# Channel mix of the last layer woven into the last attention unit

## The chip, the cores and the metric

One core of a Trainium2 chip runs the whole program. The metric is the device time of one execution in microseconds (us). TensorE (PE) multiplies matrices, VectorE (DVE), ScalarE (ACT) and GpSimd (POOL) work on tiles, SyncE (SP) issues DMAs.

## The reference

Two layers on x, 2048 tokens by 128 channels. Each layer has a modulated layer norm, attention with a gated residual, another modulated layer norm and a feed-forward part with a gated residual. Layer 0 has 16 heads of 8 and a mixture of 16 experts. Layer 1 has causal attention with 8 heads of 16 and a channel mix:

```
h = layernorm(x) * (1 + cb) + sb
h_prev = h shifted by one token (zeros in front)
xr = mu_r * h + (1 - mu_r) * h_prev
xk = mu_k * h + (1 - mu_k) * h_prev
x = x + gb * sigmoid(xr @ W_r.T) * (square(relu(xk @ W_k.T)) @ W_v.T)
```

The channel mix is the last thing computed; its result is the output. It goes along tokens only by the shift by one, so 512 tokens of it need the attention of those tokens, and one column of the block in front of them.

## The kernel before

x stays in SBUF as 16 tiles of 128 tokens by 128 channels. Work on tokens goes by 4 blocks (0 to 3) of 512 tokens (`QB`), each of 4 tiles (`TB`). Transposed activations lie as 128 channels by 2048 tokens.

Attention (`attention`) goes by units: a unit is one block of 512 queries and one group of 4 heads. Layer 1 has 8 units (0 to 7), two for each block; units 6 and 7 belong to block 3. A unit has two passes.

- The first pass (`first_pass`) multiplies queries by keys into a PSUM tile of 128 x 1024 (L411), and VectorE takes the maximum from it (L415; on the diagonal L420, which masks). At its end the negated maxima are made (L426, L436, L437), transposed on TensorE (L444) and copied (L445).
- The second pass (`second_pass`) multiplies keys by queries again (L476), adds the negated maxima with a second product (L482), ScalarE takes the exponential out of PSUM (L486), on the diagonal GpSimd clears the later tokens (L489), and TensorE weighs the values with it (L502) into a PSUM bank `av`.

The first pass of the next unit runs ahead within the second pass of the present one (`look_ahead`), so the last unit, 7, has no first pass beside it. Both passes take their score tiles from one ring of three (`ps_s`). Of the two further banks, one is the `av` of the unit and the other (`other_bank`) serves every small product. What a unit leaves behind, `normalise`, goes into a list `late` of pieces: `divide` (transposes L533, reciprocal and product L537, L538), and after the second unit of a block `turn_back` (L545, L548) and `project` (four products L554 and the addition to x, L558). A piece is taken from `late` at every second step of a second pass, and at every step in the last unit. A step is one score tile; unit 7 has 32.

Behind attention comes the channel mix for all four blocks. `layernorm_T` takes the statistics of 16 tiles (L180, L181), one square root on ScalarE (L182), reciprocal (L183), 16 normalised tiles (L189), 16 transposes (L191), and four evictions on ScalarE (L192). Then, for each block, two scalings on ScalarE (L1208), two additions of the shifted tile on VectorE (L1210), products with W_r and W_k (L1213, L1215), the sigmoid on ScalarE (L1217), the maximum with 0 on VectorE (L1219), the square on GpSimd (L1221), the product with W_v (L1223), times the sigmoid (L1225), times the gate on GpSimd (L1226), four transposes back (L265), the addition to x (L267) and a DMA of 256 KB to the output (L1228).

Inside layer 1's attention and the channel mix, the order of instructions on each engine is decided by the framework's scheduler when the program is built, from the order in which the kernel calls them and from what depends on what. Every engine then runs its list in order, and an instruction that waits holds up all behind it on that engine.

Of the kernel before, what the change touches and what calls it, by code (L numbers as in the profile page):

```python
# [19 lines left out]
P = 128  # L20
# [23 lines left out]
def two_layers(ctx: ExitStack, tc: tile.TileContext, a: dict, out: bass.AP):  # L44
# [126 lines left out]
    def layernorm_T(hT, off, scale, shift, tagp):  # L171

        with tc.tile_pool(name=tagp + "_s", bufs=1) as one, \
                tc.tile_pool(name=tagp + "_w", bufs=4) as wp, \
                tc.tile_pool(name=tagp + "_p", bufs=4, space=PSUM) as pp:
            stats = one.tile([P, NT, nc.vector.BN_STATS_DIM], F32, name=tagp + "stats", tag="stats")
            mv = one.tile([P, NT, nc.vector.BN_AGGR_DIM], F32, name=tagp + "mv", tag="mv")
            rstd = one.tile([P, NT], F32, name=tagp + "rstd", tag="rstd")
            for t in range(NT):
                nc.vector.bn_stats(stats[:, t, :], x[:, t, :])  # L180
                nc.vector.bn_aggr(mv[:, t, :], stats[:, t, :])  # L181
            nc.scalar.activation(rstd, mv[:, :, 1], AF.Sqrt, bias=eps)  # L182
            nc.vector.reciprocal(rstd, rstd)  # L183
            for b in range(NB):
                ps = pp.tile([P, QB], F32, name=f"{tagp}ps{b}", tag="ps")
                for i in range(TB):
                    t = b * TB + i
                    xn = wp.tile([P, P], F32, name=f"{tagp}xn{t}", tag="xn")
                    nc.vector.tensor_scalar(xn, x[:, t, :], mv[:, t, 0:1], rstd[:, t:t + 1],  # L189
                                            ALU.subtract, ALU.mult)  # L190
                    nc.tensor.transpose(ps[:, i * P:(i + 1) * P], xn, ident)  # L191
                nc.scalar.activation(hT[:, off + b * QB:off + (b + 1) * QB], ps, AF.Identity,  # L192
                                     bias=shift, scale=scale)

# [66 lines left out]

    def add_to_x(b, t, ps):

        for i in range(TB):
            nc.tensor.transpose(ps[:, i * P:(i + 1) * P], t[:, i * P:(i + 1) * P], ident)  # L265
        xb = x[:, b * TB:(b + 1) * TB, :]
        nc.vector.tensor_tensor(xb, xb, ps.rearrange("p (t c) -> p t c", c=P), ALU.add)  # L267
# [49 lines left out]
    def attention(layer, hT, ngrp, dk, scale, causal, kvp, begin, prepare, wq, bq, folded, ended,  # L317
# [23 lines left out]
        with ExitStack() as s:  # L341
# [116 lines left out]
            def second_pass(u):  # L458
# [48 lines left out]
                def steps():  # L507
# [10 lines left out]
                    weights.append(lambda: (last(), late.extend(normalise(u, av))))  # L518
# [3 lines left out]
            def normalise(u, av):  # L522
# [28 lines left out]
                def project():  # L551
                    ps = other_bank()
                    for i in range(TB):
                        nc.tensor.matmul(ps[:, i * P:(i + 1) * P],  # L554
                                         attended[b][:, i * P:(i + 1) * P], folded[0],
                                         start=True, stop=True)
                    xb = x[:, b * TB:(b + 1) * TB, :]
                    nc.vector.tensor_tensor(xb, xb, ps.rearrange("p (t c) -> p t c", c=P), ALU.add)  # L558
# [50 lines left out]
            for u in range(len(units)):  # L609
# [3 lines left out]
                for n in range(1, size + 1):  # L613
# [5 lines left out]
                    if n == LEAD and u + 1 == len(units):  # L619
# [327 lines left out]
    with ExitStack() as s:  # L947
# [214 lines left out]
        while len(shared) > 1:  # L1162
# [22 lines left out]

    attention(1, h2, H1 // HG, D1, float(P) ** -0.5, True, pool1,
              lambda ep, pp, stacks: ((lambda st: kS1), (lambda kt, head: vA1[:, kt, :]), qS1),
              ready1, wq1, None, folded1, lambda bank: [], lambda late, *_: late)
    a1.close()


    h = hpool.tile([P, HOFF + T], F32, name="hT3", tag="hT")
    nc.gpsimd.memset(h[:, 0:HOFF], 0.0)
    layernorm_T(h, HOFF, m[:, 4:5], m[:, 3:4], "ln3")
    ov = out.rearrange("(t p) c -> p t c", p=P)
    with ExitStack() as s:
        rp = s.enter_context(tc.tile_pool(name="mixc", bufs=1))
# [96 lines left out]
```

## Time and profile before

| | |
|---|---|
| median of 3 runs | 1252.55 us (1251.54 to 1255.32) |
| the profiled execution | 1254.59 us, its span 1252.9 us |
| TensorE busy, share of the span | 92% |
| VectorE busy | 75% |
| ScalarE busy | 62% |
| GpSimd busy | 8% |
| granted TensorE clock, mean | 0.944 |
| unit 7 begins, by its first L476 | 1170.2 us |
| last L502 of unit 7 ends | 1209.55 us |
| last addition to x ends | 1249.2 us |

Times in the profile are from the start of the span. An engine is busy while an instruction runs on it; the number behind an operation is the time of one or, with x and a count, of a run of them. The idle time in brackets is that of the engine just before, with the instruction that ended it.

### The profile page before, as it was taken

Reading aid. Unit: us, or ns where it says so; the run is one execution under the profiler, and the core shown is the slowest. Engines: PE = TensorE matmul, PEld = TensorE weight load, DVE = VectorE, ACT = ScalarE, POOL = GpSimd, SP = SyncE. Lnnn points to the kernel's source line nnn. Section 1 sums busy time; section 2 is a strip of 40 time slices with the busy share of each in tenths; the row PEclk is TensorE's granted clock in tenths of the full one; section 3 lists DMA queues with packets and bytes.
Section 4 is the critical chain, followed back from the end, with each engine's and each line's share of the span. In section 5 each row is a group of like instructions: output and inputs, shape, how many; then the busy total and the mean of one; then the engine's idle time right before and its main releaser. Section 6 shows DMA issues by size and latency. Waiting matters only on the chain.

```text
span 1252.9 us, 22356 instructions
## 1 busy us (share of the span) xinstructions
PE 1156.8 (92%) x9230; PEld 523.6 (42%) x9230; DVE 943.9 (75%) x1462; ACT 780.3 (62%) x853; POOL 94.4 (8%) x157
## 2 busy tenths in 40 slices
PE   4579999999999999999999999979978989999985
PEld 2233434444343443443344333447734444444432
DVE  3888898889889889889889983343378788897134
ACT  6107777777777777777777778743333455656763
POOL 2002000000000000000000000320232011110113
PEclk9658999999999999999999999999977899999987
DMA  4841010203220213110000000032210101000001
GB/s 122 112 52 35 2 52 1 70 27 77 69 69 12 59 36 98 38 52 2 1 3 2 1 2 2 20 122 76 66 45 7 35 1 35 1 1 2 2 1 34
DMA packets 63094, 45.22 MB, mean 36 GB/s; under 512 B 6608, under 2 KB 56912, under 8 KB 62480
## 3 DMA queue, kind: packets, MB, share of 16 engines
q1 hardware_dynamic: 60224, 40.37, 13.2%
q0 software_dynamic: 1024, 2.10, 0.6%
q10 hardware_dynamic: 1744, 1.32, 0.6%
q8 instruction: 73, 1.20, 0.4%
q14 instruction: 29, 0.24, 0.1%
HBM read 9.88 MB, written 21.95 MB: 25 GB/s over the span
## 4 chain that ended last, share of the span: by engine, by line
PE 82%; DVE 10%; ACT 4%; issue 1%; DMA 1%; POOL 1%; ACTq 0%; POOLq 0%; DVEq 0%
PE a0bank L502 24%; PE a0p L476 17%; PE a0p L411 13%; PE a1bank L502 5%; PE a1p L476 4%; DVE a0mx L415 3%; DVE a1mx L415 2%; PE a1p L411 2%; PE a1p L482 2%; PE sg L991 2%; DVE a1masked L420 2%; ACT a0e L486 1%; PE gu L1043 1%; PE a0bank L533 1%; PE sum L979 1%
## 5 line engine op out<-in xcount | busy, mean ns | idle before, releaser
L415 DVE TENSOR_REDUCE a0mx<-a0p 128x2 f32<-128x1024 f32 x512 | 624.0, 1225 | 75.9 <-PE a0p L411 66.5
L486 ACT ACTIVATE a0e<-a0p 128x1024 f32<-128x1024 f32 x512 | 522.6, 1025 | 171.9 <-PE a0p L476 146.2
L502 PE MATMUL a0bank<-a0e,vA 128*32 128x256 f32 x4096 | 333.4, 392 | 0.8 <-ACT a0e L486 0.8
L411 PE MATMUL a0p<-kS,a0qS 64*128 64x512 f32 x1024 | 248.1, 480 | 24.7 <-DVE a0mx L415 13.0
L476 PE MATMUL a0p<-a0qS,kS 64*128 64x512 f32 x1024 | 260.6, 498 | 0.0
L486 ACT ACTIVATE a1e<-a1p 128x1024 f32<-128x1024 f32 (+3 forms) x160 | 143.1, 897 | 97.6 <-PE a1p L482 92.3
L476 PEld LDWEIGHTS a0p<-a0qS,kS 64*128 64x128 f32 x1024 | 97.3, 184 | 204.5 <-issue 128.7
L411 PEld LDWEIGHTS a0p<-kS,a0qS 64*128 64x128 f32 x1024 | 100.3, 192 | 109.4 <-ACT a0e L486 56.8
L502 PEld LDWEIGHTS a0bank<-a0e,vA 128*32 128x32 f32 x4096 | 86.4, 108 | 137.9 <-issue 124.4
L415 DVE TENSOR_REDUCE a1mx<-a1p 128x2 f32<-128x1024 f32 x96 | 115.8, 1222 | 17.8 <-PE a1p L411 17.2
L502 PE MATMUL a1bank<-a1e,vA 128*32 128x256 f32 (+1 forms) x1152 | 96.9, 385 | 0.4 <-POOL a1e L489 0.4
L476 PE MATMUL a1p<-a1qS,kS 64*128 64x512 f32 (+3 forms) x320 | 76.3, 463 | 4.9 <-DVE a1mx L415 3.7
L411 PE MATMUL a1p<-kS,a1qS 64*128 64x512 f32 (+3 forms) x320 | 67.7, 422 | 11.2 <-DVE a1mx L420 4.4
L420 DVE CUSTOM_DVE_ANT_0 a1masked<-a1p,later 128x128 f32<-128x128 f32 (+3 forms) x128 | 62.6, 489 | 13.4 <-PE a1p L411 7.5
L799 POOL DMA_INDIRECT sent<-hs,row_i x16 | 15.9, 995 | 712.6 <-DVE ln11xn L252 689.5
L482 PE MATMUL a1p<-a1mT,a1ones 64*128 64x512 f32 (+3 forms) x320 | 62.2, 375 | 0.0
L476 PEld LDWEIGHTS a1p<-a1qS,kS 64*128 64x128 f32 x320 | 31.5, 189 | 61.6 <-issue 32.3
L411 PEld LDWEIGHTS a1p<-kS,a1qS 64*128 64x128 f32 x320 | 32.2, 195 | 39.5 <-DVE a1mx L420 11.5
L489 POOL TENSOR_SCALAR_AFFINE_SELECT a1e<-a1e 128x256 f32<-128x256 f32 x64 | 26.0, 406 | 255.4 <-ACT a1e L486 255.4
L502 PEld LDWEIGHTS a1bank<-a1e,vA 128*32 128x32 f32 x1152 | 25.8, 109 | 42.8 <-issue 32.6
L445 ACT CAST a0mT<-a0bank 8x512 fp32r<-8x512 f32 x16 | 9.2, 576 | 45.4 <-PE a0bank L444 45.4
L482 PEld LDWEIGHTS a1p<-a1mT,a1ones 64*128 64x128 f32 x320 | 32.2, 193 | 2.3 <-issue 1.7
(340 smaller groups left out, 718.2 us busy)
## 6 DMA issues: line engine op xcount, KB each, us to landing
sent<-blank SPq DMA_DIRECT2D x68, 256.0 KB
kS<-a0qS SPq DMA_DIRECT2D x28, 128.0 KB
wgu_sb<-in_gate_up SPq DMA_DIRECT2D x1, 2048.0 KB
a0qS<-a0qh SPq DMA_DIRECT2D x62, 32.0 KB
a0qS<-a0ql SPq DMA_DIRECT2D x62, 32.0 KB
xs<-sent SPq DMA_DIRECT2D x31, 64.0 KB
y_rows<-y SPq DMA_DIRECT2D x7, 256.0 KB
a1qS<-a1qh SPq DMA_DIRECT2D x24, 64.0 KB
```

The costliest lines, as they stand in the source:

```text
L411: nc.tensor.matmul(ps[:, j, :n], qS[b][r:r + RT, st, i * P:(i + 1) * P], kS(st)[r:r + RT, kb * QB:kb * QB + n], start=True, stop=True)
L415: nc.vector.tensor_reduce(pm[:, i, 2 * pair:2 * pair + 2, kb], ps, AX.X, ALU.max)
L420: nc.vector.tensor_tensor_reduce(masked[:, :n], ps[:, j, :n], later[:, QB - n:], 1.0, LOWEST, ALU.add, ALU.max, pm[:, i, g, kb:kb + 1])
L476: nc.tensor.matmul(ps[:, j, q0:], kS(st)[r:r + RT, kt * P:(kt + 1) * P], qS[b][r:r + RT, st, q0:], start=True, stop=fused)
L482: nc.tensor.matmul(ps[:, j, q0:], ones[r:r + RT, g // S, :], shift[u][r:r + RT, q0:], start=False, stop=True)
L486: nc.scalar.activation(e[:, :, q0:], ps[:, :, q0:], AF.Exp, scale=scale)
L489: nc.gpsimd.affine_select(out=e[:, :, q0:q0 + P], in_=e[:, :, q0:q0 + P], compare_op=ALU.is_ge, fill=0.0, base=0, pattern=[[0, 2], [1, P]] ...
L502: nc.tensor.matmul(av[g * W:(g + 1) * W, c0:c1], vA(kt, grp * HG + g), held[kt, g // 2][:, g % 2, c0:c1], start=(kt == 0 and c0 == 0), sto ...
L533: nc.tensor.transpose(ps[:, i * P:(i + 1) * P], o[:, i * P:(i + 1) * P], ident)
L799: nc.gpsimd.indirect_dma_start(out=sent[t], in_=hs[:, i, :], in_offset=None, out_offset=bass.IndirectOffsetOnAxis(ap=row_i.bitcast(U32)[:, ...
L979: nc.tensor.matmul(sums[b][:, i * P:(i + 1) * P], act[:, i * P:(i + 1) * P], wsd[:, k, :], start=(k == 0 and i == 0), stop=(k == NS - 1), ...
L991: nc.tensor.matmul(ps[:, j, :], w[:, k * P:(k + 1) * P], hT[:, b * QB:(b + 1) * QB], start=True, stop=True)
```

## The change

The channel mix gets a class `mix` with one object for each block. For blocks 0, 1 and 2 its steps are pieces in `late`, put there by the new function `early` at step 2 of unit 7 (before: `ended` at step 8, with nothing for this layer). For block 3 they come behind unit 7 in `last1`. What a block does is rewritten:

- The reciprocal root of the variance of blocks 0 to 2 is by Newton steps on VectorE (12 small instructions for a block); block 3 keeps the square root on ScalarE, with both table changes (square root, hyperbolic tangent) called for ahead of their use.
- Blocks 0 to 2: eviction of the transposed norm, both scalings, both additions and the maximum are on VectorE; the square stays on GpSimd. Block 3: eviction and one scaling on ScalarE, square on VectorE.
- The sigmoid becomes 0.5 * (1 + tanh(z / 2)); 0.5 and the gate are multiplied into W_v once (`fold_value`). The gate's own instruction falls away.
- The products with W_r and W_v are four of 128 x 128 with the tokens as the stationary side, so the result already has tokens as rows. The four transposes back fall away.
- For block 3 the addition of the attention to x goes by 4 tiles, and the end of the mix (product with tanh, addition, DMA) by two halves.
- All small products of the pieces use `other_bank`. Pieces of `normalise` go to the front of `late` in layer 1.

```diff
                     last = weights.pop()
-                    weights.append(lambda: (last(), late.extend(normalise(u, av))))
+                    def ending():
+                        last()
+                        where = 0 if causal and u + 1 < len(units) else len(late)
+                        late[where:where] = normalise(u, av)
+                    weights.append(ending)
...
-                    xb = x[:, b * TB:(b + 1) * TB, :]
-                    nc.vector.tensor_tensor(xb, xb, ps.rearrange("p (t c) -> p t c", c=P), ALU.add)
+                    parts = TB if causal and b == NB - 1 else 1
+                    for i in range(parts):
...
-                    if n == LEAD and u + 1 == len(units):
+                    if n == (2 if causal else LEAD) and u + 1 == len(units):
                         late.extend(ended(other_bank))
...
+    def fold_value(ps):
+        nc.tensor.matmul(ps[:, :P], m[:, 5:6].to_broadcast([P, P]), ident, start=True, stop=True)
+        nc.vector.scalar_tensor_tensor(wfvg, wfv, 0.5, ps[:, :P], ALU.mult, ALU.mult)
+
+    class mix:
...
+        def begin(self):
+            name = f"ln3{self.b}"
+            mv, steps = statistics(self.b, name)
+            y, more = newton(mv, name)
+            self.xn = lnp.tile([P, TB, P], F32, name=name + "xn", tag="xn")
+            return steps + more + [lambda: normal(self.b, name, mv, y, self.xn)]
+        def mixed(self, i, engine=None):
+            t = self.t[i] = wp.tile([P, QB], F32, name=f"mt{self.b}{i}", tag=f"mt{i}")
+            if engine is None:
+                nc.vector.tensor_scalar_mul(t, self.now, vcol(V_MUR + i))
+            else:
+                nc.scalar.activation(t, self.now, AF.Copy, scale=vcol(V_MUR + i))
+            nc.vector.scalar_tensor_tensor(t, self.before, rest[:, i:i + 1], t, ALU.mult, ALU.add)
+        def receptance(self, ps):
+            for i in range(TB):
+                cols = slice(i * P, (i + 1) * P)
+                nc.tensor.matmul(ps[:, cols], self.t[0][:, cols], wfr, start=True, stop=True)
+            self.r = wp.tile([P, QB], F32, name=f"mr{self.b}", tag="mr")
+            nc.scalar.activation(self.r, ps, AF.Tanh, scale=0.5)
+        def key(self, ps):
+            nc.tensor.matmul(ps, wfk, self.t[1], start=True, stop=True)
+            self.k = wp.tile([P, QB], F32, name=f"mk{self.b}", tag="mk")
+            nc.vector.tensor_scalar_max(self.k, ps, 0.0)
+        def square(self, engine):
+            engine.tensor_tensor(self.k, self.k, self.k, ALU.mult)
+        def value(self, ps, parts=1):
+            for i in range(TB):
+                cols = slice(i * P, (i + 1) * P)
+                nc.tensor.matmul(ps[:, cols], self.k[:, cols], wfvg, start=True, stop=True)
+            for i in range(parts):
...
+                nc.vector.scalar_tensor_tensor(r, r, 1.0, ps[:, cols], ALU.add, ALU.mult)
+                nc.vector.tensor_tensor(x[:, ts, :], x[:, ts, :],
+                                        r.rearrange("p (t c) -> p t c", c=P), ALU.add)
+                nc.sync.dma_start(out=ov[:, ts, :], in_=x[:, ts, :])
+
+    def early(bank):
+        def evicted(b):
+            ps = bank()
+            for i in range(TB):
+                nc.tensor.transpose(ps[:, i * P:(i + 1) * P], b.xn[:, i, :], ident)
+            nc.vector.tensor_scalar(b.now, ps, m[:, 4:5], m[:, 3:4], ALU.mult, ALU.add)
...
+        pieces = [lambda: fold_value(bank())]
+        for n in range(NB):
+            b, last = blocks[n % (NB - 1)], blocks[n - 1]
+            front = [lambda b=b: begin(b), lambda b=b: evicted(b),
+                     lambda b=b: (b.mixed(1), b.mixed(0))]
+            products = [lambda b=last: (b.key(bank()), b.square(nc.gpsimd)),
+                        lambda b=last: b.receptance(bank()), lambda b=last: b.value(bank())]
+            if n == 0:
+                pieces += front
+            elif n < NB - 1:
+                pieces += [products[0], front[0], products[1], front[1], products[2], front[2]]
+            else:
+                pieces += [products[0], lambda: None, products[1], lambda: None, products[2]]
+        return pieces
+
+    def last1(late, bank, ps_s, ep):
...
+        return late[:-1] + [lambda: table(AF.Sqrt), late[-1], begin,
+                       lambda: turn_normal(bank(), b.xn, b.now, m[:, 4:5], m[:, 3:4]),
+                       lambda: (b.mixed(1), b.mixed(0, nc.scalar)),
+                       lambda: b.key(banks[0]),
+                       lambda: b.receptance(banks[1]),
+                       lambda: b.square(nc.vector), lambda: b.value(banks[2], 2)]
...
-              ready1, wq1, None, folded1, lambda bank: [], lambda late, *_: late)
+              ready1, wq1, None, folded1, early, last1)
```

In the instruction lists of the changed kernel as built, TensorE's products of the pieces lie in unit 7, one for every one to two steps, with nine score tiles still to come behind the last of them. The scheduler puts the statistics, the Newton steps and the normalised tiles earlier on VectorE: block 0's into unit 3's second pass and unit 4's first, block 1's into unit 4's second pass and unit 5's first, block 2's statistics and Newton steps into unit 6's second pass and unit 7's first. TensorE's list ahead of unit 7 is the same but for one product that changes place with its neighbour.

## The prediction

> **What bounds the kernel now.** The question is what unit 7, in which the pieces are put, has to spare, and what the stretch behind it costs. I read the busy time by stretches first (columns: stretch, length, busy us and count of PE, PEld, DVE, ACT, POOL, granted clock, DMA share, GB/s):
>
> ```profile
> 1010.00:1035.00 25.00, 21.92 (x186) 10.71 (x182) 21.95 (x59) 12.68 (x17) 2.90 (x5) 1.00 0.00 1
> 1135.00:1160.00 25.00, 25.00 (x240) 11.46 (x241) 19.16 (x30) 16.80 (x18) 0.00 (x0) 1.00 0.01 2
> 1177.00:1210.00 33.00, 32.16 (x337) 12.33 (x329) 0.39 (x2) 25.49 (x28) 3.25 (x8) 1.00 0.01 2
> 1210.00:1253.00 43.00, 24.31 (x72) 12.09 (x72) 23.79 (x72) 14.04 (x21) 11.67 (x8) 0.73 0.09 25
> ```
>
> In unit 7 (third row) TensorE is full and VectorE does nothing; behind it (last row) no engine is full, and the engines wait for each other in a chain. Ahead of unit 7 VectorE has little left. Then the timeline: a step of unit 7, the first of the mix, and its end.
>
> ```profile
> 1198.52 0.64 PE L502 MATMUL a1bank<-a1e,vA 128*32 128x256 f32 x8
> 1199.09 0.49 PE L476 MATMUL a1p<-a1qS,kS 64*128 64x512 f32 x2
> 1199.43 0.40 PE L482 MATMUL a1p<-a1mT,a1ones 64*128 64x512 f32 x2
> 1199.75 0.64 PE L502 MATMUL a1bank<-a1e,vA 128*32 128x256 f32 x8
> ...
> 1209.61 0.49 DVE L180 BATCH_NORM_STATS2 ln3stats<-x 128x6 f32<-128x128 f32 x2 [33.49 <-PE a1bank L502]
> ...
> 1215.33 0.69 DVE L558 TENSOR_TENSOR x<-x,a1bank 128x512 f32<-128x512 f32 x1 [1.70 <-PE a1bank L554]
> ...
> 1248.51 0.69 DVE L267 TENSOR_TENSOR x<-x,px 128x512 f32<-128x512 f32 x1 [2.87 <-PE px L265]
> ```
>
> A step is 1.23 us (1198.52 to 1199.75) with no gap on TensorE, so all that TensorE gets in addition there lengthens unit 7. From the last product of unit 7 (1209.55) to the end of the span (1252.9) pass 43.35 us. Last, VectorE around block 2's addition:
>
> ```profile
> 1139.40 0.69 DVE L558 TENSOR_TENSOR x<-x,a1bank 128x512 f32<-128x512 f32 x1
> 1140.77 1.23 DVE L415 TENSOR_REDUCE a1mx<-a1p 128x2 f32<-128x1024 f32 x1 [0.68 <-PE a1p L411]
> 1142.23 1.23 DVE L415 TENSOR_REDUCE a1mx<-a1p 128x2 f32<-128x1024 f32 x1 [0.24 <-PE a1p L411]
> ```
>
> Each step of 1.47 us leaves VectorE 0.24 us, and here the scheduler puts block 2's statistics.
>
> **Part 1: the stretch behind unit 7 (saves 21.9).** Now only block 3 is there. Counted from the last L502:
> - Up to the attention's addition nothing changes (copy, L533, L537, L538, L545, L548, L554): 1215.33 - 1209.55 = 5.8. Three of the four tile additions run while L554 still works on later tiles; the fourth, 128 columns, takes 0.3 by the line through L538 (256 columns, 0.42) and L558 (512, 0.69). Statistics of four tiles took 1.22 (1216.05 to 1217.27): 7.3.
> - Square root 0.31, reciprocal about 0.2: 7.8. From the first normalised tile to the eviction's start, ln20 at 910.50 needed 1.67 (912.17), eviction 0.78: 10.3.
> - The scaling on VectorE, 512 columns SBUF to SBUF, has no row. Bounds: 0.35 (L189, 128 columns) and 0.68 (L1110, an addition of 512); 0.5, between. The shifted addition 0.75: 11.6.
> - W_k's product: 1.13 at full clock, 2.08 at half (L295 at 913.00). The profile shows the clock halving at 1212.8 and staying there to 1222.8, so I take half, 13.6. Maximum and square, 0.69 each with hops: 15.1. In TensorE's list W_r's four products stand between; at half clock four such took 2.07 (L554 at 1213.12), which ends at 15.4.
> - W_v's four products: 2.07 or, at full clock, 1.10; I take 1.6, since it is the first work that could meet a full clock: 17.0. Two halves of product and addition (256 columns, 0.42 each, overlapped): 18.2.
> - From the last addition to the end passed 3.7 (1249.2 to 1252.9); half the bytes, 3.3: 21.5.
>
> Saving 43.35 - 21.5 = 21.85; 20.3 to 23 by those ends. The clock changes at 1212.8, 1222.8, 1226.2, 1229.6 and 1243.2, multiples of 3.4 apart. The Trainium skill (TensorE: Matmul & The Clock Gate, Part 1) gives windows of about 3.4 us, and full clock only after a busy one; the trace agrees. By it W_v's products would be at half clock and the end 0.5 later.
>
> The table change to the tangent is called between square root and eviction: 1.28 (L1217's load), then 0.2 (L1160): 7.6 + 1.5 = 9.1, ahead of the eviction's start at 9.5, so I cost it at nothing; without that cover it would be 1.5. The Trainium skill (ScalarE: Activation LUTs, What ACT_TABLE_LOAD costs) says a change costs about 2.66 us with the flush around it, by which the eviction would start 0.8 later. The trace differs: at 924.33 the next activation starts within 0.02 of a load that took 1.28.
>
> **Part 2: unit 7 becomes longer (costs 11.2).** TensorE gets 3 x 4 transposes at 0.58 (L444 at 1163.82, next at 1164.40) = 1.74; 3 products with W_k at 1.05 (L295, 1020.48 to 1021.53) = 3.15; 6 sets of four products, at 1.09 by the next start (L554, 1061.17 to 1062.26) and 1.03 by the growth of the step, 1.06 x 6 = 6.36. The gate's fold stands where TensorE waits 0.80 for a copy on ScalarE (L533 at 1174.64): nothing, or 0.3 if that wait is gone. Sum 11.2; 10 to 13.
>
> What else the pieces issue lies under that. VectorE gets about 16 us (for a block eviction and maximum 0.69, two scalings 0.5, two shifted additions 0.75, the end 0.75 + 0.69) in 44 us where it did 0.39. ScalarE, 25.5 of 33, gets 3 tangents of 0.6 in its list between exponentials. GpSimd's three squares (1.04 to 1.48, L1221) are ahead of the eight L489 in its list, which come in the last quarter. The three DMAs of 256 KB on SP's queue have nothing behind them but block 3's.
>
> **Part 3: the normalisation moves ahead of unit 7 (costs 5.2).** The old statistics cost nothing separate from part 1. For each block now: statistics 1.22, twelve Newton instructions at 0.2 (ln23's, 1012.88 to 1013.86), 2.4, and four normalised tiles at 0.26, 1.05. They stand ahead of maxima in VectorE's list; TensorE waits there for a free score tile, and behind it all second passes.
> - Block 2: 3.6 (its tiles are normalised in unit 7) among five maxima. Gone against the 0.68 and four times 0.24 above, and the 0.69 from a maximum's end (1142.00) to when TensorE needs its tile (1142.69): 1.3 lost.
> - Block 1: 4.65, between 1063.15 and 1074.2, where VectorE idles 0.62, 0.30 and 5 x 0.24, in sum 2.1. No float is left at the end: TensorE already waits 0.53 there for the negated maxima (L437): 2.4 lost.
> - Block 0: between 1007.4 and 1018.5 VectorE has no gap. Statistics and half the Newton steps go in there, interleaved with ln23's of the same kind, which hides their dependences: 1.5 lost. The rest meets idle times of 0.80 (1022.4) and 1.45 (1028.7): nothing, or 1.75 if those fill up.
>
> Sum 5.2. Ends: 0, if all is taken up by later waits, and 12.9, all that is inserted.
>
> **Sum.** -21.85 + 11.2 + 5.2 = -5.4. The profiled execution took 1254.59 (span 1252.9, 1.7 around it) and would take 1249.2, span 1247.5. It lies 2.0 over the median of the runs; against that, 1252.55, the forecast is 1247.1.
>
> **Rivals.**
> - *VectorE is the bound ahead of unit 7* and all 12.9 is lost: -21.85 + 11.2 + 12.9 = +2.3, 1254.8, no change to speak of. For it: the first row, VectorE and TensorE both 88% busy. Against: 1135 to 1160, VectorE 77%.
> - *One spare bank.* Slower: all 13 uses of the pieces go through `other_bank`. If TensorE reaches each before VectorE or ScalarE has evicted the last, every use waits up to an eviction and a hop, 0.69 + 0.1: 10.3, so +4.9, 1257.4. It decides the sign from 0.42 for each use. For it: L502 waited 0.42 at 1176.18 for such a bank. Against: in the built list at least a step's products, 1.2, stand between two uses, and mostly two steps.
> - *The insertion is free:* TensorE's own later waits take it up, and the sum is -10.7, 1241.9. For it: TensorE waits several times for ScalarE or GpSimd there. Against: TensorE is 98 to 100% busy from 1060 on.
> - That the change doesn't do what it says can be seen from the built list: the products are in unit 7; only the statistics aren't.
>
> **How the numbers follow.** A measurement here tells about 0.3%, 3.8 us. Forecast (1244 to 1250) 0.57, all lost 0.20, spare bank 0.10, free 0.13. Within the forecast, parts 1 and 2 at their bad ends leave less than 3.8; I count 0.05 of it as no change, and 0.03 of the second case as slower. Faster 0.65, same 0.22, slower 0.13. The range reaches down into the free case and up to the second, 1241.5 to 1254, leaving out the fourth part of the free case and most of the spare bank.
>
> **What would show it.** In the changed trace: unit 7's step still 1.23 where no piece stands, the unit 50 to 51 long instead of 39.4; block 3's stretch 21 to 22 from the last weighing product to the end; at blocks 0, 1 and 2 statistics, waits of TensorE for maxima that add up to about 5. Wrong would be waits of the products in unit 7 for evictions, a unit over 54, or the start of unit 7 later by over 9 us or under 2.

## The result, and the profile after

The changed kernel takes 1245.63 us (median of 6 runs, 1244.76 to 1246.26) where the kernel before took 1253.07 beside it: a ratio of 0.9938, 95% interval 0.9925 to 0.9951, 7.4 us less. The forecast was 1247.1, 5.4 less. The profiled execution took 1246.13, with a span of 1244.4 (1254.59 and 1252.9 before). All lines of the program moved: L445 is the old L476 (score), L380 the old L411, L384 the old L415 (maximum), L471 the old L502 (weighing), L530 the old L554, L537 the old L558.

The busy time by stretches, in the columns of the prediction (stretch, length, busy us and count of PE, PEld, DVE, ACT, POOL, granted clock, DMA share, GB/s):

```profile
1010.00:1035.00 25.00, 22.45 (x184) 10.47 (x182) 24.17 (x78) 12.96 (x16) 2.50 (x4) 1.00 0.01 2
1135.00:1160.00 25.00, 24.64 (x236) 11.51 (x236) 21.30 (x50) 16.56 (x18) 0.00 (x0) 1.00 0.01 2
1178.64:1211.70 33.06, 33.06 (x282) 15.73 (x278) 13.96 (x26) 20.24 (x21) 3.12 (x3) 1.00 0.06 18
1222.00:1244.40 22.40, 9.95 (x46) 7.06 (x38) 8.69 (x28) 6.54 (x10) 0.00 (x0) 0.64 0.04 12
```

In unit 7 (third row) TensorE is still busy without a gap, and VectorE, which did 0.39 us there, now does 13.96. Ahead of it (first and second row) VectorE does 2.2 us more in each 25. The stretch behind unit 7 is half as long, and there TensorE runs at a mean clock of 0.64.

TensorE in unit 7: its first scores, one round of pieces and its last weighing product (the timeline, TensorE alone; between scores, the second products L451 and the weighing products L471 are left out):

```profile
1171.39 0.45 PE L445 MATMUL a1p<-a1qS,kS 64*128 64x512 f32 x2
...
1178.64 0.50 PE L445 MATMUL a1p<-a1qS,kS 64*128 64x512 f32 x2
1179.87 0.51 PE L445 MATMUL a1p<-a1qS,kS 64*128 64x512 f32 x2
1180.54 1.12 PE L1213 MATMUL a1bank<-mt,wfk_sb 128*128 128x512 f32 x2
1182.17 0.49 PE L445 MATMUL a1p<-a1qS,kS 64*128 64x512 f32 x2
1183.40 0.50 PE L445 MATMUL a1p<-a1qS,kS 64*128 64x512 f32 x2
1184.06 1.16 PE L1208 MATMUL a1bank<-wfr_sb,mt 128*128 128x128 f32 x8
1185.72 0.50 PE L445 MATMUL a1p<-a1qS,kS 64*128 64x512 f32 x2
1186.39 0.66 PE L1240 MATMUL a1bank<-ident,ln31xn 128*128 128x128 f32 x4
1187.54 0.50 PE L445 MATMUL a1p<-a1qS,kS 64*128 64x512 f32 x2
...
1221.75 0.43 PE L471 MATMUL a1bank<-a1e,vA 128*32 128x128 f32 x8 [0.39 <-POOL a1e L458]
```

A step without a piece takes 1.23 (1178.64 to 1179.87), as before. With W_k's product it takes 2.30, with W_r's four 2.32, with the transposes 1.82: 1.07, 1.09 and 0.59 more, and each of them just its own length on TensorE. From its first score to its last weighing product unit 7 takes 50.8 (1171.39 to 1222.18) where it took 39.35: 11.4 more. TensorE stands still twice in it, 0.41 for a copy and 0.39 for GpSimd, and for no eviction of a piece.

Behind unit 7, block 3's chain (the timeline; in square brackets idle time before, and what ended it):

```profile
1225.68 2.07 PE L530 MATMUL a1bank<-a1wog,a1onT 128*128 128x128 f32 x8 [0.68 <-ACT a1onT L524]
1227.86 0.88 DVE L537 TENSOR_TENSOR x<-x,a1bank 128x128 f32<-128x128 f32 x4 [3.57 <-PE a1bank L530]
1228.66 0.48 DVE L180 BATCH_NORM_STATS2 ln33stats<-x 128x6 f32<-128x128 f32 x2
...
1229.91 0.30 ACT L193 ACTIVATE ln33y<-ln33mv,eps 128x4 f32<-128x4 f32 x1 [2.76 <-DVE ln33mv L181]
1230.22 1.28 ACT L1271 ACT_TABLE_LOAD   x1
...
1232.13 0.78 ACT L236 ACTIVATE hT<-a1bank,mod 128x512 f32<-128x512 f32 x1 [0.41 <-PE a1bank L235]
...
1232.94 0.49 DVE L1200 TENSOR_SCALAR mt<-hT,vec_sb 128x512 f32<-128x512 f32 x1 [1.38 <-ACT hT L236]
...
1234.36 2.05 PE L1213 MATMUL mixps<-mt,wfk_sb 128*128 128x512 f32 x2 [2.27 <-DVE mt L1203]
...
1238.08 1.42 PE L1223 MATMUL mixps<-wfvg,mk 128*128 128x128 f32 x8
...
1239.62 0.75 DVE L1229 SCALAR_TENSOR_TENSOR mr<-mr,mixps 128x256 f32<-128x256 f32 x2 [1.68 <-PE mixps L1223]
1240.29 0.75 DVE L1230 TENSOR_TENSOR x<-x,mr 128x256 f32<-128x256 f32 x2
```

From the last weighing product to the end of the span pass 22.2 us (1222.18 to 1244.4), where 43.35 passed: 21.1 less. The four additions begin only when all of L530 is done (1225.68 + 2.07 = 1227.75). W_k's product takes 2.05 at half clock.

Ahead of unit 7 the sum needs care, since executions differ in when layer 1 begins at all: the first unit's joined maxima (a1nx) start at 936.84 before, at 935.86 after, and between 934.08 and 937.23 in the traces of the first four experiments below. So I count from there to unit 7's joined maxima: 226.20 before (936.84 to 1163.04), 228.36 after (935.86 to 1164.22), 2.16 more. The four lines, before and after:

```profile
936.84 0.18 DVE L426 TENSOR_REDUCE a1nx<-a1mx 128x16 f32<-128x16 f32 x1
...
1163.04 0.22 DVE L426 TENSOR_REDUCE a1nx<-a1mx 128x16 f32<-128x64 f32 x1
```

```profile
935.86 0.18 DVE L395 TENSOR_REDUCE a1nx<-a1mx 128x16 f32<-128x16 f32 x1
...
1164.22 0.22 DVE L395 TENSOR_REDUCE a1nx<-a1mx 128x16 f32<-128x64 f32 x1
```

To unit 4 it is 104.81 and 104.86, to unit 5 137.32 and 139.30. Block 1's normalisation, which stands between units 4 and 5, costs 1.9; block 0's, ahead of unit 4, about nothing; block 2's, ahead of unit 7, 0.2. What block 1's costs is seen at the weight loads of the scores, which wait for maxima:

```profile
1068.32 0.18 PEld L445 LDWEIGHTS a1p<-a1qS,kS 64*128 64x128 f32 x2 [0.70 <-DVE a1mx L384]
1070.11 0.19 PEld L445 LDWEIGHTS a1p<-a1qS,kS 64*128 64x128 f32 x2 [0.74 <-DVE a1mx L384]
1072.01 0.19 PEld L445 LDWEIGHTS a1p<-a1qS,kS 64*128 64x128 f32 x2 [0.85 <-DVE a1mx L384]
```

Before, that load was idle for 0.41 at this place, for its issue alone:

```profile
1068.62 0.19 PEld L476 LDWEIGHTS a1p<-a1qS,kS 64*128 64x128 f32 x2 [0.41 <-issue]
```

Around block 2 VectorE is late too, but has caught up by 1154 (the timeline, VectorE):

```profile
1142.00 1.21 DVE L384 TENSOR_REDUCE a1mx<-a1p 128x2 f32<-128x1024 f32 x1
...
1143.67 1.22 DVE L384 TENSOR_REDUCE a1mx<-a1p 128x2 f32<-128x1024 f32 x1
...
1153.87 1.23 DVE L384 TENSOR_REDUCE a1mx<-a1p 128x2 f32<-128x1024 f32 x1 [0.24 <-PE a1p L380]
```

The maxima follow at 1.67 in the place of 1.47, and from 1153.87 VectorE idles 0.24 ahead of each again.

The sum: +2.2 ahead of unit 7, +11.4 in it, -21.1 behind it, -7.5 together, against 7.4 between the medians. The two spans differ by 8.5, since this execution of the changed kernel also began layer 1 1.0 earlier.

### The profile page after: what moved, and what is told of

Read it like the earlier page. It is cut to its first block, busy times and chain, and to the rows that moved or that the text cites. A ratio compares the mean times of both kernels' runs of the same rounds, so it can differ in the third digit from the quotient of the medians.

```text
span 1244.4 us, 22459 instructions
## 1 busy us (share of the span) xinstructions
PE 1155.9 (93%) x9264; PEld 527.9 (42%) x9264; DVE 951.9 (76%) x1515; ACT 774.2 (62%) x845; POOL 85.9 (7%) x152
## 4 chain that ended last, share of the span: by engine, by line
PE 81%; DVE 12%; ACT 4%; DMA 1%; issue 1%; SPq 0%; DVEq 0%; ACTq 0%; POOLq 0%; POOL 0%
PE a0bank L471 24%; PE a0p L445 17%; PE a0p L380 13%; PE a1bank L471 5%; PE a1p L445 4%; DVE a0mx L384 3%; DVE a1mx L384 3%; PE a1p L380 2%; PE a1p L451 2%; DVE a1masked L389 2%; PE sg L972 2%; ACT a0e L455 1%; PE gu L1024 1%; PE a0bank L509 1%; PE sum L960 1%
## 5 line engine op out<-in xcount | busy, mean ns | idle before, releaser
L384 DVE TENSOR_REDUCE a0mx<-a0p 128x2 f32<-128x1024 f32 x512 | 623.8, 1224 | 74.6 <-PE a0p L380 64.9
L471 PE MATMUL a0bank<-a0e,vA 128*32 128x256 f32 x4096 | 333.3, 391 | 0.8 <-ACT a0e L455 0.8
L380 PE MATMUL a0p<-kS,a0qS 64*128 64x512 f32 x1024 | 248.0, 480 | 23.6 <-DVE a0mx L384 13.1
L445 PE MATMUL a0p<-a0qS,kS 64*128 64x512 f32 x1024 | 260.5, 497 | 0.0
L445 PEld LDWEIGHTS a0p<-a0qS,kS 64*128 64x128 f32 x1024 | 97.3, 184 | 204.5 <-issue 129.5
L380 PEld LDWEIGHTS a0p<-kS,a0qS 64*128 64x128 f32 x1024 | 100.3, 192 | 108.4 <-ACT a0e L455 56.8
L471 PEld LDWEIGHTS a0bank<-a0e,vA 128*32 128x32 f32 x4096 | 86.3, 108 | 137.4 <-issue 123.8
L384 DVE TENSOR_REDUCE a1mx<-a1p 128x2 f32<-128x1024 f32 x96 | 115.7, 1220 | 14.8 <-PE a1p L380 14.4
L471 PE MATMUL a1bank<-a1e,vA 128*32 128x256 f32 (+1 forms) x1152 | 97.1, 385 | 0.4 <-POOL a1e L458 0.4
L445 PE MATMUL a1p<-a1qS,kS 64*128 64x512 f32 (+3 forms) x320 | 76.6, 465 | 5.4 <-DVE a1mx L384 4.2
L380 PE MATMUL a1p<-kS,a1qS 64*128 64x512 f32 (+3 forms) x320 | 67.8, 423 | 11.5 <-DVE a1mx L389 4.6
L451 PE MATMUL a1p<-a1mT,a1ones 64*128 64x512 f32 (+3 forms) x320 | 61.7, 375 | 0.0
L445 PEld LDWEIGHTS a1p<-a1qS,kS 64*128 64x128 f32 x320 | 31.5, 189 | 63.3 <-issue 24.8
L380 PEld LDWEIGHTS a1p<-kS,a1qS 64*128 64x128 f32 x320 | 32.2, 195 | 39.9 <-DVE a1mx L389 11.6
L471 PEld LDWEIGHTS a1bank<-a1e,vA 128*32 128x32 f32 x1152 | 25.7, 108 | 42.5 <-issue 35.2
L451 PEld LDWEIGHTS a1p<-a1mT,a1ones 64*128 64x128 f32 x320 | 32.0, 193 | 1.8 <-issue 1.3
```

The costliest lines, as they stand in the source:

```text
L380: nc.tensor.matmul(ps[:, j, :n], qS[b][r:r + RT, st, i * P:(i + 1) * P], kS(st)[r:r + RT, kb * QB:kb * QB + n], start=True, stop=True)
L384: nc.vector.tensor_reduce(pm[:, i, 2 * pair:2 * pair + 2, kb], ps, AX.X, ALU.max)
L445: nc.tensor.matmul(ps[:, j, q0:], kS(st)[r:r + RT, kt * P:(kt + 1) * P], qS[b][r:r + RT, st, q0:], start=True, stop=fused)
L451: nc.tensor.matmul(ps[:, j, q0:], ones[r:r + RT, g // S, :], shift[u][r:r + RT, q0:], start=False, stop=True)
L471: nc.tensor.matmul(av[g * W:(g + 1) * W, c0:c1], vA(kt, grp * HG + g), held[kt, g // 2][:, g % 2, c0:c1], start=(kt == 0 and c0 == 0), sto ...
```

## The experiments

On the chips of all runs from the fifth on, the kernel before takes 1263 to 1264, so times are compared there as ratios to it, and traces by three stretches: layer 1's first passes (from the first unit's joined maxima to unit 7's; 226.2 before, 228.4 after), unit 7 (from its transposes of the maxima to the copy of its sums; 57.2 after) and the end (from that copy to the end of the span; 22.2 after). The interval of a ratio is some 0.2% to either side, 2.5 us, so by their times most of these kernels can't be told from the changed one; a difference of a stretch is that of one trace against another.

**Normalisation of blocks 0 to 2 left out**

```
-            for step in b.begin():
-                step()
+            b.xn = x[:, b.b * TB:(b.b + 1) * TB, :]
```

> Leaves out the normalisation of blocks 0, 1 and 2 of layer 1's mix (their statistics, Newton steps and normalised tiles, 12.9 us of VectorE); their transposes take x itself, so these blocks' output is not the reference's. All else is as in the changed kernel. Theory of the forecast (the work costs 5.2 us where it was moved to): unit 7 begins 5.2 earlier than in the changed kernel's trace and the time is 1240.4. Theory of the two traces (blocks 0 and 2 cost 0.2 each, block 1 costs 1.9): unit 7 begins 2.1 to 2.3 earlier, of which 1.9 at block 1, and the time is about 1243.5. Rival (the 1.0 us by which layer 1 began earlier in the changed kernel's trace belongs to the change): without the normalisation layer 1 begins as in the kernel before, and the time is 1244.5.

Measured: 1243.54, ratio 0.9916 (0.9896 to 0.9936). First passes 225.96 (936.01 to 1161.97), 2.40 less than in the changed kernel, of which 1.9 fell at block 1; unit 7 57.2, the end 22.3. Of the 12.9 us by which VectorE was charged, 2.4 are paid. Layer 1 began at 936.01, so its earlier start is not the normalisation's doing.

**Statistics and Newton steps twice**

```
+            mv, steps = statistics(b.b, f"again{b.b}")
+            for step in steps + newton(mv, f"again{b.b}")[1]:
+                step()
```

> Statistics and Newton steps of blocks 0, 1 and 2 are computed twice, once for nobody: 3.6 us more of VectorE for each block, 10.8 in all, ahead of unit 7. Theory of the forecast (a fixed share is lost, 5.2 of 12.9): 4.4 us more, 1250.0. Theory of idle time (VectorE lags behind and catches up in the idle time that follows, and only what is beyond that is lost): block 1, which has used it up, loses all 3.6; block 2 has about 1.2 us of idle time left up to the end of unit 6's first pass and loses 2.4; block 0 has some 1.5 to 3 up to unit 4's middle and loses 0.6 to 2.1: 6.6 to 8.1 more, 1252.2 to 1253.7. Rival (free, TensorE's later waits take it up): under 1 more.

Measured: 1246.43 (1244.53 to 1250.81), ratio 0.9948 (0.9928 to 0.9968). First passes 231.36 (936.58 to 1167.94), 3.0 more than in the changed kernel: 1.7 at block 0, 0.9 at block 1, the rest behind. The median is only 0.8 above the changed kernel's and the traced execution one of the longest, so that the times alone would also fit the rival (under 1). By the trace no theory had it; mine of idle time (6.6 to 8.1) missed by the most. One reason stands in the trace, and it is already in the changed kernel's own, where block 0's steps alternate with those of ln23, and block 1's stand alone (start, us):

```profile
1013.91 0.16 DVE L218 TENSOR_TENSOR ln23t<-ln23v,ln23y 128x4 f32<-128x4 f32 x1
1013.99 0.16 DVE L218 TENSOR_TENSOR ln30t<-ln30v,ln30y 128x4 f32<-128x4 f32 x1
...
1066.58 0.16 DVE L220 SCALAR_TENSOR_TENSOR ln31y<-ln31t,ln31y 128x4 f32<-128x4 f32 x1
1066.77 0.16 DVE L218 TENSOR_TENSOR ln31t<-ln31v,ln31y 128x4 f32<-128x4 f32 x1
```

A step that needs the one before it starts 0.19 behind it, one that doesn't 0.08. The price of 0.2 is that of a dependence and not of work, and in this run's trace the second copy's steps stand in part in the first one's gaps. How much of the 3.6 to 5.1 us that are missing that makes was not measured.

**Normalisation kept in unit 7**

```
+                if kept:
+                    tc.keep_in_program_order(ins)      # each bn_stats of blocks 0 to 2
...
+        pieces = [lambda: begin(blocks[0]), lambda: fold_value(bank()), nothing, nothing,
+                  lambda: evicted(blocks[0]), lambda: mixed(0)]   # mixed(n) also begins block n + 1
```

> The statistics of blocks 0, 1 and 2 are pinned behind what VectorE has before them in the program, and so the normalisation stands in unit 7, where VectorE has room; the pieces' order is changed so that at least three steps lie between a block's statistics and its transposes. The work is the same. Theory of the traces: unit 7 begins 2.1 to 2.3 earlier than in the changed kernel, unit 7 is as long (50.8), the time is 1243.5. Theory of the forecast: 5.2 earlier, 1240.4. Rival (in unit 7 the normalisation delays evictions and maxima of the pieces, and TensorE waits for the spare bank): unit 7 is 2 us or more longer and nothing is gained, 1245.5 or more.

Measured: 1243.42, ratio 0.9914 (0.9895 to 0.9933). First passes 225.80 (934.08 to 1159.88), 2.56 less; unit 7 58.0, 0.7 more. Most of that is one wait, at block 1's transposes:

```profile
1184.38 1.12 DVE L230 TENSOR_SCALAR ln31xn<-x,ln31mv,ln31y 128x128 f32<-128x128 f32 x4
1184.88 1.01 PE L1242 MATMUL a1bank<-ident,ln31xn 128*128 128x128 f32 x4
```

The four transposes take 1.01 for 0.66, at the pace of the normalised tiles, and that step takes 2.38 for 1.82. So the place ahead of unit 7 costs 2.4 to 2.6, and 1.8 of it is had back here.

**Two pieces in each step**

```
-                    if late and (n % 2 == 1 or u + 1 == len(units)):
-                        late.pop(0)()
+                    for _ in range(2 if causal and u + 1 == len(units) else 1):
+                        if late and (n % 2 == 1 or u + 1 == len(units)):
+                            late.pop(0)()
```

> Two pieces in each step of unit 7 in the place of one: the same work on every engine, but a piece has half the time until the next that needs its bank or its result. It puts a price on the rival of the forecast that all pieces go through one spare bank. If the bank's turn-around is hidden by the step between two pieces alone, TensorE now waits within unit 7 for VectorE and ScalarE, up to an eviction and a hop, 0.8 us, for half of the 13 uses, 5 us, and as much again for the chain from eviction to shifted addition to product, in all 5 to 10 us more than the changed kernel: 1251 to 1256. If two uses one behind the other cost nothing (TensorE's queue runs ahead far enough): unchanged, 1245.6.

Measured: 1247.57, ratio 0.9950 (0.9930 to 0.9970). First passes 228.36, as in the changed kernel; unit 7 59.3, 2.1 more. The waits are of the expected kind (0.43 ahead of a product with W_r for VectorE's shifted addition, 0.7 of a weight load for the tangent), but less than half in sum: the list that is built spreads the pieces again. The rival of the one spare bank, 10.3 in the forecast, is 0 at the changed kernel's spacing and 2.1 at this one.

**Own PSUM tiles for block 3's parts**

```
-                    ps = other_bank()
+                    pss = [other_bank()] + [
+                        ps_s.tile([P, 2, QB], F32, name=f"{L}pr{i}", tag="s")[:, 0, :]
+                        for i in range(1, parts)]
...
-                       lambda: b.square(nc.vector), lambda: b.value(banks[2], 2)]
+                       lambda: b.square(nc.vector), lambda: b.value(mixps(2), bank())]
```

> Block 3's four products with the folded output weights go to four PSUM tiles in the place of four parts of one, and its two halves with W_v to two tiles. Theory (VectorE's first addition waited for all four products because it waits for the tile that they share, not for its own part; so the additions by tiles and the end in halves hid nothing): three additions now run beside the products, the last ends 0.3 behind them in the place of 0.9, and at the end the first half's addition runs beside the second half's products: 0.6 and 0.5 less, from the copy of unit 7's sums to the end 21.1 in the place of 22.2, the time 1244.5. Rival (something else holds the first addition, the products' own end or VectorE's order): unchanged, 1245.6.

Measured: ratio 0.9935 (0.9914 to 0.9957); the end takes 21.5, where 21.1 was expected. The additions and the end's halves, from its timeline:

```profile
1240.02 0.80 PE L534 MATMUL a1bank<-a1wog,a1onT 128*128 128x128 f32 x2 [0.68 <-ACT a1onT L524]
...
1240.61 1.49 PE L534 MATMUL a1pr<-a1wog,a1onT 128*128 128x128 f32 x6
1240.85 0.29 DVE L539 TENSOR_TENSOR x<-x,a1bank 128x128 f32<-128x128 f32 x1 [2.22 <-PE a1bank L534]
...
1241.28 1.14 DVE L539 TENSOR_TENSOR x<-x,a1pr 128x128 f32<-128x128 f32 x3
1242.34 0.48 DVE L180 BATCH_NORM_STATS2 ln33stats<-x 128x6 f32<-128x128 f32 x2
...
1253.07 0.42 DVE L1232 SCALAR_TENSOR_TENSOR mr<-mr,mixps 128x256 f32<-128x256 f32 x1 [1.45 <-PE mixps L1226]
1253.65 0.42 DVE L1232 SCALAR_TENSOR_TENSOR mr<-mr,a1bank 128x256 f32<-128x256 f32 x1 [0.15 <-PE a1bank L1226]
```

With a tile of its own each addition follows its own product, and three run beside the rest. From the first product to the statistics pass 2.32 (2.98 in the changed kernel). So it was the sharing that held them: in the changed kernel's trace only the first of the four additions waits for TensorE, and it waits for all the products. The four tiles lie in four PSUM banks as well, so it is open whether an addition waits for the tile or for the bank. The halves overlap as well (the second waits 0.15 behind its product), but here their products ran at half clock up to 1253.27, which took the gain back: 2.97 from W_v's first product to the last addition, 2.96 in the changed kernel. Weighed against the Trainium skill (Perfetto Trace Analysis, Matmuls), independent groups should rotate through PSUM banks so that the reading of one overlaps the products of the next: the additions agree, by 0.66.

**One addition, one end**

```
-                    parts = TB if causal and b == NB - 1 else 1
+                    parts = 1
...
-                       lambda: b.square(nc.vector), lambda: b.value(banks[2], 2)]
+                       lambda: b.square(nc.vector), lambda: b.value(banks[2])]
```

> Block 3's addition is one instruction again and its end is in one part; all else is as in the changed kernel. Theory (neither hides anything): the additions take 0.69 in the place of 0.88, 0.2 less; the end has one product and one addition, 1.44, as long as the two halves took from first start to last end (1.42), and then twice the bytes, 0.3 more. In sum 0.1 more, 1245.7. Theory of the forecast (three of the four additions run beside the products, the halves overlap): 0.4 more at the additions, and at the end 0.6 to 0.9 more, 1246.6 to 1246.9.

Measured, one run: the end takes 22.6, 0.4 more. From L530's start to the statistics 2.90 (2.98 in the changed kernel), so four additions bring nothing; from W_v's first product to the end of the span 6.8 for 6.3, of which the product's own length is 0.15. The halves are worth 0.3, and all of it is the half of the bytes (from the last addition to the end 3.7 for 3.4); from the end of W_v's products to that of the last addition pass 1.53 and 1.54, so they don't overlap.

**TensorE kept at work behind unit 7**

```
+        def warm(n):
+            for _ in range(n):
+                tc.keep_in_program_order(nc.tensor.matmul(
+                    idle[:, :P], wfk, h3[:, HOFF:HOFF + P], start=True, stop=True))
```

> Behind unit 7 TensorE gets 22 products of 128 columns that nobody reads, in the gaps between block 3's steps: two behind each of the two transposes, ten behind the products with the output weights, eight behind the transposes of the normalised tiles. Theory (in these gaps the granted clock falls to half, and block 3's products take twice as long for that reason): the clock stays at 1.00 to the products with W_v, the products with the output weights take 1.1 for 2.07, that with W_k 1.05 for 2.05, those with W_v 1.1 for 1.42, the transposes end 0.2 earlier: 2.5 less, from the copy to the end 19.7, the time 1243.1. Rival (a product that nobody reads is in the way of one that is needed, 0.27 at each of five places, or the clock falls all the same): 1.3 more to unchanged, 1245.6 to 1246.9.

Measured: ratio 0.9927 (0.9904 to 0.9949), which by itself can't be told from the changed kernel; the trace can. The end takes 19.9, 2.3 less, and the clock falls only at 1250.90, when the products are over:

```profile
1237.56 1.16 PE L530 MATMUL a1bank<-a1wog,a1onT 128*128 128x128 f32 x8 [0.23 <-ACT a1onT L524]
...
1245.19 1.10 PE L1214 MATMUL mixps<-mt,wfk_sb 128*128 128x512 f32 x2 [0.48 <-DVE mt L1204]
...
1247.96 1.13 PE L1224 MATMUL mixps<-wfvg,mk 128*128 128x128 f32 x8 [0.78 <-DVE mk L1219]
```

1.16, 1.10 and 1.13 for 2.07, 2.05 and 1.42: with the transposes of the normalised tiles (1.10 for 1.24), the half clock was 2.3 of block 3's 22. Against an end whose clock falls late (21.0, last section) the gain is 1.1.

**Block 2's last products behind unit 7**

```
-                pieces += [products[0], lambda: None, products[1], lambda: None, products[2]]
+                pieces += [products[0]]
...
+        return [lambda: (got.append(mixps(3)), c.received(got[0], 0, 2)), divide,
+                lambda: c.received(got[0], 2, TB), turn_back, gate, ...
```

> Block 2's products with W_r and W_v, 2.1 us of TensorE, leave unit 7 and stand between block 3's steps behind it; block 2's addition and its DMA follow at the end. Theory (unit 7 is TensorE's bound and pays each product in full, while behind it TensorE, VectorE and ScalarE wait for each other and have room): unit 7 is 2.1 shorter, the stretch behind it is as long as before (22.2) or up to 1 shorter, since gaps that are filled keep the clock up for longer; the time is 1242.5 to 1243.5. Rival (each product put in a gap delays the next step of block 3's chain, and block 2's addition and transfer delay the end): the stretch is 2 or more longer, 1245.6 or more.

Measured: ratio 0.9906 (0.9886 to 0.9926). Unit 7 takes 55.3, 2.0 less for 2.1 us of products, and the end 21.2, 1.0 less, with the products of L530 at full clock (1.16). Ends with nothing put into them are as short where the clock's windows lie well (21.0, last section), so the 1.0 can't be put down to the filled gaps. What leaves unit 7 is saved nearly in full, and behind it there is room: the end is no longer than the changed kernel's, and 0.2 longer than those.

**Only the weaving undone**

```
+        unwoven.extend(pieces[1:])
+        return pieces[:1]
...
+        return late + unwoven + [lambda: table(AF.Sqrt), begin,
```

> Only the weaving is undone: the pieces of blocks 0, 1 and 2 are the same and in the same order, but all but the gate's fold stand behind unit 7, among block 3's steps, on three rotating PSUM tiles; the tangents stand ahead of block 3's root, so that no table is loaded more often. Theory (in unit 7 TensorE pays for each piece in full, so the weaving hides VectorE's, ScalarE's and GpSimd's share and not TensorE's; behind unit 7 VectorE, 8.7 us busy of 22.2 in the changed kernel, gets 16 more and becomes what the stretch waits for): unit 7 is 11.4 shorter, 45.8 from its transposes to the copy of its sums for 57.2; the stretch behind it takes 33 to 37 for 22.2; the time is 1245 to 1249, so that the weaving is worth 0 to 3 and the rest of the change's gain is the new form. Rival (the weaving is what brings the gain): the stretch takes 40 or more, nearly that of the kernel before (43.4), and the time is 1252 or more.

Measured: ratio 0.9972 (0.9956 to 0.9988). Unit 7 takes 46.2, 11.1 less; the end 37.6, 15.4 more: 4.3 us slower than the changed kernel. That lies between the two theories: 0.6 above the 33 to 37 of the first, 2.4 below the 40 of the rival. Of the change's 7.5 us the weaving brings 4.3, more than the 0 to 3 expected, and the new form of the mix the other 3.2. What is undone is not all: the normalisation of blocks 0 and 1, and block 2's statistics and Newton steps, stand ahead of unit 7 in this trace too (block 0's from 1021.2, block 1's from 1074.0, block 2's from 1152.5), and what they cost is in both kernels.

**The edits together**

Kept normalisation, own tiles, block 2's last products behind unit 7, TensorE kept at work; then the same with one step more ahead of the transposes of blocks 1 and 2, beside the changed kernel.

```
-                pieces += [lambda b=b: b.receptance(bank()), nothing,
+                pieces += [lambda b=b: b.receptance(bank()), nothing, nothing,
```

> Four edits together: the normalisation of blocks 0 to 2 kept in unit 7; block 3's products with the output weights in four PSUM tiles and its end in two; block 2's products with W_r and W_v behind unit 7; products that nobody reads in TensorE's gaps behind unit 7. If their single gains add up, each as read from its trace against the changed kernel's (unit 7 begins 2.5 earlier and is 0.7 longer; additions 0.7; unit 7 2.0 shorter; clock 2.3, from which 0.3 goes for what full clock takes from the gain at the end's halves), the sum is 6.5: unit 7's copy 3.8 earlier and the stretch behind it 19.2 or less for 22.2, the ratio to the kernel before 0.9886, 1239 on the chip of the first runs. Rival (block 2's addition and the products that nobody reads get in each other's and block 3's way): the stretch is over 20.5, the ratio 0.990 or more.

> As the four edits together, with one step more between the normalisation of blocks 1 and 2 and their transposes, since TensorE waited 0.56 in unit 7 at block 1's transposes for the last normalised tile. Theory: unit 7 takes 55.3 from its transposes to the copy of its sums for 56.0 (57.2 in the changed kernel); layer 1 up to unit 7 takes 225.9 from the first unit's maxima to unit 7's, where the run of the four edits took 228.2, because the clock halved for 7 us in unit 4 behind a wait of 1.8; the stretch behind unit 7 stays at 19.0; the time is 7 to 8 less than the changed kernel's in the same job. Rival (the clock's fall in unit 4 belongs to the edits): it falls there again, and the time is 5.5 to 6.5 less.

> The changed kernel itself, beside the four edits on the same chip. Its ratio to the kernel before was 0.9938 on the chip of the first runs; if the gain in microseconds is what carries over (7.4), it is 0.994 here too. From the first unit's maxima to unit 7's 228.4 to 229.4, unit 7 57.2, the stretch behind it 21 to 22.3, by where the clock's windows fall.

Measured: the first 0.9903 (0.9883 to 0.9924) where 0.9886 was expected, the second 0.9885 (0.9860 to 0.9910) and, beside the second, the changed kernel 0.9923 (0.9900 to 0.9946): 1248.73 against 1254.15, 5.4 less. (The changed kernel gains 9.4 there on the kernel before, more than the 7.4 that it was expected to keep.) The stretches of the second against the changed kernel's there: first passes 228.5 and 229.3, unit 7 55.4 and 57.2, the end 19.0 and 22.3, 5.9 less in sum (the intervals overlap at their ends). Unit 7 and the end came as expected. The first passes didn't: the first of the two versions took 228.2 and the second 228.5, for 225.9. In unit 4 the clock fell, in both (the second version, by windows of 3.4):

```profile
1019.90:1023.30 3.40, 1.90 (x20) 0.84 (x18) 3.15 (x15) 0.85 (x3) 1.22 (x3) 0.99 0.00 0
1023.30:1026.70 3.40, 3.08 (x16) 1.53 (x18) 3.40 (x7) 1.02 (x1) 0.90 (x1) 0.50 0.02 5
1026.70:1030.10 3.40, 3.40 (x18) 2.20 (x16) 2.15 (x6) 1.80 (x2) 0.37 (x1) 0.50 0.00 0
```

A window in which TensorE worked 1.90 of 3.40 is followed by two at half clock. It holds 1.46 of a wait of 1.82 for maxima (up to its edge at 1023.26), and the window behind it holds the other 0.36. From unit 3's joined maxima to unit 4's pass 41.3 for 40.1. So the rival's 5.5 to 6.5 was nearer. The changed kernel on that chip waits 1.46 there, nearly all of it in one window, and has one window at half clock; so have the other traces of these chips without the kept normalisation. On the first chip neither the kernel before, which waits 1.82 as well, nor the version with the kept normalisation showed any: a window's edge lies within the wait there (at 1014.56 before, where the wait is from 1013.53 to 1015.35), and TensorE works at least 2.2 in either window. So it goes with the place of the windows, and not with the length of the wait, whether the clock falls here at all. Whether the longer wait or its place makes the second window at half clock is open.

## Why the prediction was right, and where its sizes were off

| Step | Predicted | Measured |
|---|---|---|
| Stretch behind unit 7 | 21.5, saves 21.85 | 22.2, saves 21.1 |
| Unit 7 | +11.2, 10 to 13 | +11.4 |
| Normalisation ahead of unit 7 | +5.2, 0 to 12.9 | +2.2 (2.4 by leaving it out) |
| Sum | -5.4 | -7.5; medians -7.4 |

Part 1 was 0.75 too hopeful and part 3 was 3.0 too dear; that the two have opposite signs is luck, and brings the sum nearer than part 3 is.

**Part 1** held in its steps but for two overlaps. The additions by tiles failed: "three of the four tile additions run while L554 still works" counted the tiles of x and not the tile in PSUM, and the additions ended 6.56 behind the last weighing product for 6.1. Own tiles got 0.66 back, so the prediction was right about the products and wrong about what the addition waits for. The statistics followed within 7.7 for 7.3, the eviction began at 9.95 for 9.5, and that 0.45 was carried to the end. The scaling without a row took 0.49 (0.5 chosen between 0.35 and 0.68). W_v's products took 1.42 for 1.6 because the clock came back within them, at 1238.69. The window before that, 1235.28 to 1238.69, is the first behind unit 7 that TensorE fills, with W_k's, W_r's and the first of W_v's products. The Trainium skill (TensorE: Matmul & The Clock Gate, Part 1) gives full clock after one busy window of about 3.4 us, and the trace agrees. That by it W_v's products would be at half clock was a wrong conclusion of the prediction: in its own times TensorE works from 11.6 on without a gap, so that a full window can end within them. Its 1212.8 for the clock's fall was 1212.53. The halves' end took 1.5 for 1.2, again with one tile for both. The table load cost nothing: 1230.22 + 1.28 = 1231.50, the next activation at 1231.52, and the eviction started at 1232.13 when its transposes were done. The Trainium skill's 2.66 for a change of table (ScalarE: Activation LUTs, What ACT_TABLE_LOAD costs) gives, as an estimate, a start at 1232.9; the trace differs.

**Part 2** held in size and reason: each piece costs its own length on TensorE, 3 x (0.59 + 1.07 + 1.09 + 1.09) = 11.5 by the steps, and taking 2.1 us of products out gave 2.0 back. The fold was free: it stands in the wait that shrank from 0.80 to 0.41.

**Part 3** is the term that was mis-sized: 2.2 for 5.2. Block 1, 2.4 predicted, was 1.9. Block 0, 1.5, was nothing: ln23's own steps had gaps of 0.1 that its steps fill, and TensorE's wait there became shorter (1.45 for 1.82). Block 2, 1.3, was 0.2: I had counted the idle time of five maxima, while VectorE went on catching up over the next ten microseconds. That a maximum is late costs only what TensorE has to wait, and it has a few tiles in hand; that is argued from the two traces, and leaving the work out (2.4) and moving it (2.6) show the size alone. The test that I set, "the start of unit 7 later by ... under 2" as a sign of error, was put in absolute time and is met (1171.39 for 1170.21, 1.2 later) through the earlier start of layer 1; counted from layer 1's first maxima it is 2.2.

**The rivals.** VectorE as the bound (12.9 lost) is out by the run without the normalisation. The spare bank cost nothing, and 2.1 at closer spacing. That the insertion is free, a sum of -10.7, was nearer in its reason than in its size: two of three blocks were free.

## What to carry to other kernels

Work that is woven into a stretch with one full engine costs that engine's share and hides the others': price it by that engine alone, and then look for a stretch in which that engine, too, has room, as the one behind unit 7 had. Parts that share a PSUM tile waited here for the whole tile: to overlap parts, give each part a tile in a bank of its own, not a slice. Price inserted work by the wait that it makes for the bound engine over the whole stretch in which the lag is made up, not over the nearest gaps, and take a chain of tiny dependent steps as latency that other work can fill.

## What the runs showed of the hardware

TensorE's granted clock changes at multiples of 3.41 us. These windows run on while the code shifts against them, and so the same instructions have different ends. Behind unit 7 the code of the end is the same in the changed kernel, in the runs without and with doubled normalisation (22.2, 22.3 and 22.3) and with the kept normalisation or the dense pieces (21.0 and 21.0). In the former the clock falls 1.8 to 3.1 us behind the copy and L530 takes 2.07; in the latter it falls 7.5 to 7.9 us behind it and L530 runs at full clock, 1.16. The half clock lasted 13.65 and 6.83 us, four windows and two. Such a difference, 1.2 us, is half of what the normalisation cost; it is why single steps are compared above beside the ends. The window need not be idle for it: 1.9 us of work in 3.4 were followed by half clock, in unit 4. No share of work shows as the limit: 1.93 in a window behind unit 7, with the normalisation kept, were followed by full clock.
